# An LSTM step cut into two halves of each quarter's units

## The chip, the cores and the metric

The kernel runs on one core of a Trainium2 chip. A core has five engines that work side by side and are held together by semaphores: TensorE (matrix products; PE in the profile, with PEld for the loading of its weights), VectorE (DVE), ScalarE (ACT), GpSimd (POOL) and SyncE (SP, which here issues the DMA transfers). The metric is the device time of one execution in microseconds (us), as a median of several runs.

## The reference, cut to what matters

The model has two layers over 32 graphs of 512 nodes with 256 features: a graph attention, a Mamba-2 block, a second graph attention, and last a recurrence (an LSTM) with gated prefix and suffix sums. The change is in the recurrence. Its inputs are swapped, so that the 512 nodes are its time steps for a batch of 32:

```python
x_proj = jnp.einsum('btd,gd->btg', x, W_ih) + b_ih + b_hh
def step(carry, xp):
    h, c = carry
    gates = xp + h @ W_hh.T
    i, f, g, o = jnp.split(gates, 4, axis=-1)
    c = jax.nn.sigmoid(f) * c + jax.nn.sigmoid(i) * jnp.tanh(g)
    h = jax.nn.sigmoid(o) * jnp.tanh(c)
    return ((h, c), h)
...
logits = jnp.einsum('bth,lh->btl', lstm_out, W_lin) + b_lin
g = argmax(logits, axis=-1)[..., None]
w = g * lstm_out
inc = jnp.cumsum(w, axis=1)
prefix = inc - w
suffix = inc[:, -1:, :] - inc
return 2.0 * lstm_out + prefix * fw_att + suffix * bw_att
```

Here `x` is the layer-normalised output of the attention, and the result is added to it. Everything is in float32.

## The kernel before, in words

**The stages.** `layers_per_batch` works through the 32 graphs and takes the first 3.4 ms; a scheduler sets the order of its instructions. Beside it, `recurrence_weights` (L1030) lays the LSTM's weights out anew, with POOL and with DMAs on SP's queue, in the first 150 us, and leaves them in DRAM as `wr`. `recurrence` (L1110) then loads them as `wall` and runs the 512 steps. At the end the sums are added to the result and written out.

**The layout of a step.** The 256 units are cut into four quarters (`Q = 4`) of `J = 64`. A tile of the recurrence has 128 partitions: quarter times 32 graphs. Along a partition lie the columns of that quarter's gates: 64 each of f, i, g, o, and two more for the logits (`W = 258`). Sigmoids are made from tanh, so that one function serves all gates; the factors of one half are in the weights.

The state `hh` of a step is turned by a VectorE transpose of blocks of 32 x 32 (L1335). Of a quarter's 64 units, the first 32 end up in the first half of the turned tile's columns and the other 32 in the second: the product's contraction in two parts `k = 0, 1` (`DK = 2`) is a sum over the first and over the second halves of all quarters' units.

**The products.** TensorE's order is written out by hand (`manual_schedule`, as for VectorE and ScalarE), and it is in order. In a step it has:

- `h_part` (L1260): turned state times `whh`, added onto what is in PSUM. There are three banks, `PARTS`: f (64 columns), i with g (128), o with the logit's columns (66). For each bank: two parts `k` times four quarters. The four quarters take 32 of the array's columns each. A float32 product stands as two records in the profile, so this is 48 records.
- `x_part` of the next step (L1250): it puts the x side of the gates into the banks by a product of `xu` with an identity (`turner`): three banks times four quarters, 24 records. Bank f has one buffer, the others two: `bufs=(1, 2, 2)`.
- in four of sixteen steps, the turn of 128 rows of normalised x (`turn`, L1174).
- one of the `units` (L1236): 128 of the 1024 gate columns of x times `wih`, for eight steps at once (256 moving columns; four records). Eight of them, one in each of eight steps, make the `xu` of a later group of eight steps. ScalarE then brings it to SBUF with its bias (L1237). The last nine steps have none.

**The chain of a step.** tanh of the three banks on ScalarE (L1320); (f + 1) c and (i + 1) g on VectorE (L1322, L1323); the new cell (L1328); its tanh on ScalarE (L1330); the state (L1333); its transpose (L1335); then the products of the next step can start.

**Beside the chain on VectorE:** g_, the state where the logit says so (L1342), the running sum `pp` (L1345), and one `extra` per step: statistics or normalisation of a later chunk's x, or a part of the results of the chunk of sixteen steps before, on 512 columns. The loop's order on VectorE is: products, cell, state, turn, g_, pp, extra.

Of the kernel before, what the change touches and what calls it, by code (L numbers as in the profile page):

```python
# [9 lines left out]
F32 = mybir.dt.float32  # L10
# [3 lines left out]
AF = mybir.ActivationFunctionType  # L14
ALU = mybir.AluOpType
# [4 lines left out]
P = 128  # L20
# [3 lines left out]
DK = D // P  # L24
# [9 lines left out]
GB = 32  # L34
CH = 16
# [994 lines left out]
def recurrence_weights(nc, pool, a, wr):  # L1030
# [4 lines left out]


    Q, J = 4, 64
    W = 4 * J + 2
    nx, nh = DK * Q * 4 * J, DK * Q * W
    n0 = nx + nh  # L1040
    half = (0.5, 0.5, 0.5, 1.0)
    for_x, for_h = (0, 3, 1, 2), (1, 0, 3, 2)

    def tile_(p, n, tag):
        return pool.tile([p, n], F32, tag=tag, name=tag)

    def ordered(raw, n, order, s):
        t = tile_(P, W, "rwt")
        nc.gpsimd.memset(t[:n, 4 * J :], 0.0)
        for to, g in enumerate(order):  # L1050
            nc.gpsimd.tensor_scalar(t[:n, to * J : (to + 1) * J], raw[:n, g * J : (g + 1) * J], half[g] * s, None, ALU.mult)
        return t
# [18 lines left out]
    nc.gpsimd.tensor_tensor(b[0][:Q], b[0][:Q], b[1][:Q], ALU.add)  # L1071
    t = ordered(b[0], Q, for_x, 1.0)
    yield
    nc.sync.dma_start(out=wr[0][:, n0 + 2 * J + 8 : n0 + 2 * J + 9], in_=bl[:, 0:1])
    nc.sync.dma_start(out=wr[1].rearrange("o (q w) -> (o q) w", q=Q), in_=t[:Q, : 4 * J])
    yield
    nc.sync.dma_start(out=wr[0][:, n0 + 2 * J : n0 + 2 * J + 8], in_=wr[1].rearrange("o (u p) -> p (o u)", p=P))
    yield
# [9 lines left out]
    for n, (src, s) in enumerate(((a.wih, 1.0), (a.whh, 0.5))):  # L1088
        for k in range(DK):
            for q in range(Q):  # L1090
                raw = tile_(P, 4 * J, f"rwraw{q % 2}")
                cols = slice(q * 4 * J, (q + 1) * 4 * J)
                if n == 0:
                    nc.sync.dma_start(out=raw, in_=src[k * P : (k + 1) * P, cols])
                else:
                    for r in range(Q):
                        r0 = r * J + k * 32
                        nc.sync.dma_start(out=raw[r * 32 : (r + 1) * 32], in_=src[r0 : r0 + 32, cols])
                yield
                t = ordered(raw, P, (for_x, for_h)[n], s)  # L1100
                if n == 1:
                    nc.gpsimd.tensor_scalar(t[:, 4 * J : 4 * J + 1], wl[:, k : k + 1], 0.5, None, ALU.mult)
                yield
                w = (4 * J, W)[n]
                o0 = n * nx + (k * Q + q) * w
                nc.sync.dma_start(out=wr[0][:, o0 : o0 + w], in_=t[:, :w])
                yield


def recurrence(ctx, tc, c, a, X3, wr, out):  # L1110
# [3 lines left out]
    nc = tc.nc  # L1114
    T = X3.shape[0]
    Q, J = 4, 64
    W = 4 * J + 2
    G = CH // 2
    wp = ctx.enter_context(tc.tile_pool(name="rw", bufs=1))
    xp_ = ctx.enter_context(tc.tile_pool(name="rx", bufs=2))  # L1120
    st = ctx.enter_context(tc.tile_pool(name="rs", bufs=3))
    ch = ctx.enter_context(tc.tile_pool(name="rc", bufs=2))
# [6 lines left out]
    n0 = nx + nh  # L1129
    wall = wp.tile([P, n0 + 2 * J + 9], F32, name="wall")  # L1130
    wih = wall[:, :nx].rearrange("p (k u c) -> p k u c", k=DK, c=P)
    whh = wall[:, nx:n0].rearrange("p (k q w) -> p k q w", k=DK, q=Q)
    fw, bw = (wall[:, n0 + n * J : n0 + (n + 1) * J] for n in range(2))
    bcol = wall[:, n0 + 2 * J : n0 + 2 * J + 8]
    level = wall[:, n0 + 2 * J + 8 :]

    turner = wp.tile([P, P + 2], F32, name="turner")
    nc.vector.memset(turner[:, P:], 0.0)
    nc.vector.tensor_copy(turner[:, :P], c.ident)

# [42 lines left out]
    def results(t0, hh, pp):  # L1183
# [42 lines left out]
        return todo + [gathered]  # L1226

    def units(t0, xT, out_, u):


        if not u:
            out_[t0] = xp_.tile([P, 2 * Q, G * GB], F32, tag="xu", name=f"xu{t0}")
        xu = out_[t0]
        pu = psx.tile([P, G * GB], F32, tag="pu", bufs=2, name=f"pu{t0}_{u}")
        for k in range(DK):
            nc.tensor.matmul(pu, wih[:, k, u, :], xT[:, k, :], start=(k == 0), stop=(k == DK - 1))  # L1236
        return lambda: nc.scalar.activation(xu[:, u, :], pu, AF.Identity, bias=bcol[:, u : u + 1])  # L1237


    PARTS = ((0, J), (J, 3 * J), (3 * J, W))  # L1240

    def x_part(t, xu):

        pg = [
            psg.tile([P, e - s], F32, tag=f"pg{n}", bufs=(1, 2, 2)[n], name=f"pg{n}_{t}") for n, (s, e) in enumerate(PARTS)
        ]
        r = (t % G) * GB
        for p, half, (s, e) in zip(pg, (1, 0, 1), ((0, J), (0, P), (J, P + 2))):
            for q in range(Q):
                nc.tensor.matmul(  # L1250
                    p[q * GB : (q + 1) * GB, :], xu[:, 2 * q + half, r : r + GB], turner[:, s:e],
                    start=True, stop=(t == 0),
                )
        return pg

    def h_part(pg, h, parts=PARTS, start=False):
        for p, (s, e) in zip(pg, parts):
            for k in range(DK):
                for q in range(Q):
                    nc.tensor.matmul(  # L1260
                        p[q * GB : (q + 1) * GB, :], h[:, k, :], whh[:, k, q, s:e],
                        start=(start and k == 0), stop=(k == DK - 1),
                    )

    with tc.manual_schedule(engines={mybir.EngineType.PE, mybir.EngineType.DVE, mybir.EngineType.Activation}):
        nxt = [None] * 2
        stats, norms, turns = normalised(0, nxt)
        for s, e in ((0, nx), (n0, n0 + 2 * J + 9), (nx, n0)):
            nc.sync.dma_start(out=wall[:, s:e], in_=wr[0][:, s:e])
# [4 lines left out]
        xu = {}  # L1274
        for u in range(2 * Q):
            units(0, nxt[0], xu, u)()
        units(G, nxt[1], xu, 0)()
        extra, turning = [], {}
        pg = x_part(0, xu[0])
        z = st.tile([P, 5 * J], F32, tag="z", name="z0")  # L1280
        nc.vector.memset(z[:, :J], 0.0)
        pp = ch.tile([P, CH + 1, J], F32, tag="pp", name="pp0")
        nc.vector.memset(pp[:, 0, :], 0.0)
        h = hh = None
        for t in range(T + 1):
# [15 lines left out]
            if last:  # L1301

                pg = [psg.tile([P, W - 3 * J], F32, tag="pg2", name="pglast")]
                h_part(pg, h, PARTS[2:], True)
            elif t:
                h_part(pg, h)
            pgs = pg
            if not last:
# [6 lines left out]
                if g < T:  # L1315
                    turned.append(units(g, (xT if g < t0 + CH else nxt)[g // G % 2], xu, u))

                for (s0, e0), p in zip(PARTS, pgs):
                    e0 = min(e0, 4 * J)
                    nc.scalar.activation(z[:, J + s0 : J + e0], p[:, : e0 - s0], AF.Tanh)  # L1320
                ab = st.tile([P, 2 * J], F32, tag="ab", name=f"ab{t}")
                nc.vector.scalar_tensor_tensor(ab[:, :J], z[:, J : 2 * J], 1.0, z[:, :J], ALU.add, ALU.mult)  # L1322
                nc.vector.scalar_tensor_tensor(  # L1323
                    ab[:, J:], z[:, 2 * J : 3 * J], 1.0, z[:, 3 * J : 4 * J], ALU.add, ALU.mult
                )
                z2 = st.tile([P, 5 * J], F32, tag="z", name=f"z{t + 1}")
                cell = z2[:, :J]
                nc.vector.scalar_tensor_tensor(cell, ab[:, :J], 0.5, ab[:, J:], ALU.mult, ALU.add)  # L1328
                tc_ = st.tile([P, J], F32, tag="tc", name=f"tc{t}")
                nc.scalar.activation(tc_, cell, AF.Tanh, scale=0.5)  # L1330
                for f in turned:
                    f()
                nc.vector.scalar_tensor_tensor(hh[:, s, :], z[:, 4 * J :], 1.0, tc_, ALU.add, ALU.mult)  # L1333
                h = st.tile([P, DK, GB], F32, tag="h", name=f"h{t}")
                nc.vector.transpose(h.rearrange("p k b -> p (k b)"), hh[:, s, :])  # L1335
                z = z2
            if t:

                i = (t - 1) % CH
                p_, h_ = (pp_was, hh_was) if s == 0 and not last else (pp, hh)  # L1340
                g_ = st.tile([P, J], F32, tag="g", name=f"g{t}")
                nc.vector.scalar_tensor_tensor(  # L1342
                    g_, pgs[-1][:, J : J + 1].to_broadcast([P, J]), level, h_[:, i, :], ALU.is_gt, ALU.mult,
                )
                nc.vector.tensor_tensor(p_[:, i + 1, :], p_[:, i, :], g_, ALU.add)  # L1345
                if s == 0 and not last:
                    nc.vector.tensor_copy(pp[:, 0, :], p_[:, CH, :])
            if extra:
                extra.pop(0)()
        assert not extra and not turning  # L1350
# [27 lines left out]
def kernel(ctx: ExitStack, tc: tile.TileContext, a, out):  # L1378
# [5 lines left out]
    X3 = dram.tile([N, nb, D], F32, name="X3")  # L1384
    wr = dram.tile([P, DK * 4 * (256 + 258) + 2 * 64 + 9], F32, name="wr"), dram.tile([1, 4 * 256], F32, name="wrb")
    odd = const.tile([1, 1], I32, name="odd")
# [78 lines left out]
```

## Time and profile before

| | us |
|---|---|
| median of 3 runs (4828.24 to 4832.57) | 4829.85 |
| the profiled execution's own time | 4838.21 |
| its span, first to last instruction | 4836.4 |
| first to last transpose of the state (512 of them) | 3398.20 to 4770.22 |
| TensorE busy in the stretch 4100 to 4300 | 196.0 of 200 |
| VectorE busy there | 152.4 |
| ScalarE busy there | 109.5 |

A line of the profile names the source line, the engine, the operation, and the tiles as out<-in with the shape, partitions x elements. In a timeline the first column is the start and the second the duration, in us; equal instructions that follow each other are one row (x48), and its duration runs to the end of the last of them. In a list of waits the numbers are: us in total, times, longest. Records of products overlap: their ends hold the way through the array, and the next product may start well before. So a busy TensorE is not one at its limit, and the starts tell more than the durations.

### The profile page before, as it was taken

How to read it: one execution, taken by the hardware profiler on the slowest of the kernel's cores; microseconds unless marked ns; L12 is line 12 of the kernel's file. 1: busy time of each engine (PE TensorE's matmuls, PEld its weight loads, DVE VectorE, ACT ScalarE, POOL GpSimd, SP SyncE). 2: the span in 40 equal slices, each digit the busy share in tenths (PEclk: the TensorE clock that was granted, in tenths of full speed). 3: DMA queues.
4: the chain of work that ended last, by engine and by line, in shares of the span. 5: the costliest groups of instructions: out<-in, count | busy, mean ns of one | idle time of the engine just before them, and what ended most of it. 6: DMA issues, size and time to landing. Idle time of an engine off the chain costs nothing. (4 is left out here: it accounts for less than half of the span.)

```text
span 4836.4 us, 126769 instructions
## 1 busy us (share of the span) xinstructions
PE 4191.4 (87%) x52926; PEld 2651.5 (55%) x52926; DVE 3279.3 (68%) x8670; ACT 3068.7 (63%) x6724; POOL 1308.8 (27%) x1012
## 2 busy tenths in 40 slices
PE   4888888888888888888888888886999999999993
PEld 2444444444554444544445444544777777777772
DVE  3567666676666666666666666664677777777776
ACT  2677667776677767677677776764555555555552
POOL 4333343333433334333343333431000000000000
PEclk7899999999999999999999999998999999999997
DMA  3221122211222112221112211111111111111115
GB/s 109 64 67 61 55 70 66 65 62 55 67 65 69 57 60 62 71 69 57 60 59 73 69 57 60 53 44 60 37 39 42 38 43 41 41 40 39 42 39 159
DMA packets 273746, 288.34 MB, mean 60 GB/s; under 512 B 152844, under 2 KB 224488, under 8 KB 270984
## 3 DMA queue, kind: packets, MB, share of 16 engines
q1 hardware_dynamic: 269784, 270.26, 19.0%
q10 hardware_dynamic: 3216, 9.81, 0.7%
q8 instruction: 418, 6.85, 0.6%
q14 instruction: 168, 1.38, 0.1%
q0 software_dynamic: 160, 0.04, 0.0%
HBM read 226.04 MB, written 37.11 MB: 54 GB/s over the span
## 5 line engine op out<-in xcount | busy, mean ns | idle before, releaser
L1260 PEld LDWEIGHTS pg<-wall,h 128*32 128x32 f32 x24528 | 476.7, 109 | 228.5 <-DVE h L1335 226.8
L1260 PE MATMUL pg<-wall,h 128*32 128x64 f32 x24528 | 561.2, 239 | 34.6 <-DVE h L1335 10.6
L1236 PE MATMUL pu<-xTr,wall 128*128 128x256 f32 x2048 | 565.5, 399 | 0.0
L467 DVE SCALAR_TENSOR_TENSOR w<-w,adjT 128x1024 f32<-128x1024 f32 x256 | 348.2, 1381 | 247.4 <-ACT w L461 247.4
L1320 ACT ACTIVATE z<-pg 128x64 f32<-128x64 f32 (+1 forms) x1536 | 345.8, 241 | 129.9 <-PE pg L1260 90.2
L1237 ACT ACTIVATE xu<-pu,wall 128x256 f32<-128x256 f32 x512 | 243.2, 475 | 278.6 <-PE pu L1236 278.6
L743 ACT ACTIVATE g<-bc,cs 128x128 f32<-128x128 f32 x1024 | 322.0, 391 | 139.7 <-PE py L811 139.7
L693 DVE SCALAR_TENSOR_TENSOR acc<-px,convw,acc 128x511 f32<-128x511 f32 (+2 forms) x480 | 347.3, 746 | 76.6 <-ACT acc L688 68.7
L461 ACT ACTIVATE w<-rb,neg,colsa 128x512 f32<-128x512 f32 x512 | 387.5, 806 | 10.2 <-DMA rb<-linea 5.8
L1236 PEld LDWEIGHTS pu<-xTr,wall 128*128 128x128 f32 x2048 | 348.8, 190 | 63.7
L533 PE MATMUL pav<-w,hb 128*64 128x512 f32 x1024 | 352.6, 615 | 21.9 <-DVE w L467 21.9
L830 PE MATMUL po<-wc,xh 128*128 128x256 f32 x1024 | 282.8, 422 | 96.8 <-POOL xh L800 96.8
L729 POOL TENSOR_TENSOR ce<-ce,cT 128x384 f32<-128x384 f32 x128 | 185.1, 1475 | 667.2 <-ACT cT L701 650.3
L54 POOL TENSOR_SCALAR ve<-mv 128x4 f32<-128x4 f32 x32 | 6.2, 193 | 1317.5 <-DVE mv L1161 1317.5
L1250 PE MATMUL pg<-turner,xu 128*32 128x64 f32 (+2 forms) x12288 | 324.3, 238 | 0.4 <-issue 0.3
L945 PE MATMUL pov<-wb,wv 128*128 128x257 f32 x1024 | 246.2, 393 | 90.4 <-DVE wv L467 90.4
L672 PE MATMUL px<-mT,win 128*128 128x512 f32 x640 | 306.9, 610 | 0.0
L830 PEld LDWEIGHTS po<-wc,xh 128*128 128x128 f32 x1024 | 203.1, 212 | 141.4 <-POOL xh L800 111.1
L1330 ACT ACTIVATE tc<-z 128x64 f32<-128x64 f32 x512 | 131.6, 257 | 224.1 <-DVE z L1328 224.1
L945 PEld LDWEIGHTS pov<-wb,wv 128*128 128x128 f32 x1024 | 193.6, 194 | 135.3 <-DVE wv L467 105.6
L1250 PEld LDWEIGHTS pg<-turner,xu 128*32 128x32 f32 x12288 | 265.6, 110 | 3.0 <-issue 1.8
L56 POOL TENSOR_TENSOR rs<-ve,mhalf 128x4 f32<-128x4 f32 (+1 forms) x192 | 256.0, 1334 | 15.9
(245 smaller groups left out, 8615.4 us busy)
## 6 DMA issues: line engine op xcount, KB each, us to landing
bc<-line SPq DMA_DIRECT2D x128, 512.0 KB
adj<-in_adj_dram SPq DMA_DIRECT2D x32, 1024.0 KB
rb<-linea SPq DMA_DIRECT2D x64, 512.0 KB
ce<-line SPq DMA_DIRECT2D x64, 384.0 KB
x<-in_x_dram SPq DMA_DIRECT2D x32, 512.0 KB
X<-x SPq DMA_DIRECT2D x32, 512.0 KB
xt<-X SPq DMA_DIRECT2D x128, 128.0 KB
x<-X SPq DMA_DIRECT2D x128, 128.0 KB
```

Source lines behind the costliest of these rows:

```text
L461: nc.scalar.activation(w[:, t, k, :], rb[:, k, :], AF.Relu, bias=neg1, scale=cols[:, 2 * m + t, h + k : h + k + 1],)
L467: nc.vector.scalar_tensor_tensor(w[:, :, k, :], w[:, :, k, :], 1.0, edges, ALU.add, ALU.mult)
L533: nc.tensor.matmul(pa[k * HO : (k + 1) * HO, :], hb[:, j, 2 * q + k, :], w[:, t, k, :], start=(j == 0), stop=(j == NT - 1),)
L672: nc.tensor.matmul(pz, win[:, k, col : col + P], mT[:, k, :], start=(k == 0), stop=(k == DK - 1))
L693: nc.vector.scalar_tensor_tensor(acc[:, s:], pz[:, : N - s], convw[:, cc, k : k + 1], acc[:, s:], ALU.mult, ALU.add)
L743: nc.scalar.activation(g[:, i, k, :], bc[:, k, i * P : (i + 1) * P], AF.Relu, bias=cs[:, i, 2 * cc + k : 2 * cc + k + 1], scale=-1.0,)
L830: nc.tensor.matmul(po[:, i * D : (i + 1) * D], xh[:, cc, it * P : (it + 1) * P], wc[:, cc, :], start=(cc == 0), stop=(cc == NC - 1),)
L945: nc.tensor.matmul(po[:, : D + 1], ws[j // 2][:, j % 2, 0, it * P : (it + 1) * P], wb[:, j, :], start=(j == 0), stop=(j == NT - 1),)
L1236: nc.tensor.matmul(pu, wih[:, k, u, :], xT[:, k, :], start=(k == 0), stop=(k == DK - 1))
L1250: nc.tensor.matmul(p[q * GB : (q + 1) * GB, :], xu[:, 2 * q + half, r : r + GB], turner[:, s:e], start=True, stop=(t == 0),)
L1260: nc.tensor.matmul(p[q * GB : (q + 1) * GB, :], h[:, k, :], whh[:, k, q, s:e], start=(start and k == 0), stop=(k == DK - 1),)
L1320: nc.scalar.activation(z[:, J + s0 : J + e0], p[:, : e0 - s0], AF.Tanh)
```

## The change

The gates of a quarter are laid out in halves: for each half of its units, g, f and i (3 x 32 columns), and then o of all 64. The banks are now: half 0 (96 columns), half 1 (96), o with the logit's columns (66). With cell, g, f, i next to each other in a tile `z[n]` of a half, (f + 1) c and (i + 1) g are one instruction. Tanh, products, cell, cell's tanh, state and turn are made by halves; `h` is now two tiles, one for each part `k`. `h_part` runs first over part 0 in the banks of both halves, then over part 1, and over bank o last. An x block of a half has 96 rows, so `xu` is now ten blocks: eight of 96 rows and two of 128 for o; blocks 8 and 9 are made beside blocks 1 and 2, so that two of eight steps have two units. The buffers of the banks are still `(1, 2, 2)`. The small tiles have two buffers instead of three, and the extra comes between g_ and pp.

```diff
-    for_x, for_h = (0, 3, 1, 2), (1, 0, 3, 2)
+    order = (3, 1, 0, 2)
...
+        halves = t[:n, : 3 * J].rearrange("p (e g j) -> p e g j", e=2, g=3)
         for to, g in enumerate(order):
-            nc.gpsimd.tensor_scalar(t[:n, to * J : (to + 1) * J], raw[:n, g * J : (g + 1) * J], half[g] * s, None, ALU.mult)
+            dst, src = t[:n, 3 * J : 4 * J], raw[:n, g * J : (g + 1) * J]
+            if to < 3:
+                dst, src = halves[:, :, to, :], src.rearrange("p (e j) -> p e j", e=2)
+            nc.gpsimd.tensor_scalar(dst, src, half[g] * s, None, ALU.mult)
...
-    nc.sync.dma_start(out=wr[0][:, n0 + 2 * J : n0 + 2 * J + 8], in_=wr[1].rearrange("o (u p) -> p (o u)", p=P))
+    c0 = n0 + 2 * J
+    nc.sync.dma_start(out=wr[0][:, c0 : c0 + 8], in_=wr[1][:, : 8 * P].rearrange("o (u p) -> p (o u)", p=P))
+    nc.sync.dma_start(out=wr[0][:96, c0 : c0 + 8], in_=wr[1][:, :no].rearrange("o (u p) -> p (o u)", p=96))
+    nc.sync.dma_start(out=wr[0][:, c0 + 8 : c0 + 10], in_=wr[1][:, no:].rearrange("o (u p) -> p (o u)", p=P))
...
+                if n == 0:
+                    o0 = k * Q * 4 * J + q * 3 * J
+                    nc.sync.dma_start(out=wr[0][:, o0 : o0 + 3 * J], in_=t[:, : 3 * J])
+                    o0 = k * Q * 4 * J + no + q * J
+                    nc.sync.dma_start(out=wr[0][:, o0 : o0 + J], in_=t[:, 3 * J : 4 * J])
...
-    st = ctx.enter_context(tc.tile_pool(name="rs", bufs=3))
+    st = ctx.enter_context(tc.tile_pool(name="rs", bufs=2))
...
+    BLOCKS = [(96 * n, 96) for n in range(2 * Q)] + [(96 * 2 * Q + P * n, P) for n in range(Q // 2)]
...
+        c0, m = BLOCKS[u]
         for k in range(DK):
-            nc.tensor.matmul(pu, wih[:, k, u, :], xT[:, k, :], start=(k == 0), stop=(k == DK - 1))
-        return lambda: nc.scalar.activation(xu[:, u, :], pu, AF.Identity, bias=bcol[:, u : u + 1])
+            nc.tensor.matmul(pu[:m], wih[:, k, c0 : c0 + m], xT[:, k, :], start=(k == 0), stop=(k == DK - 1))
+        return lambda: nc.scalar.activation(xu[:m, u, :], pu[:m], AF.Identity, bias=bcol[:m, u : u + 1])
...
-    PARTS = ((0, J), (J, 3 * J), (3 * J, W))
+    PARTS = ((0, 3 * H), (3 * H, 6 * H), (6 * H, W))
...
             psg.tile([P, e - s], F32, tag=f"pg{n}", bufs=(1, 2, 2)[n], name=f"pg{n}_{t}") for n, (s, e) in enumerate(PARTS)
         ]
         r = (t % G) * GB
-        for p, half, (s, e) in zip(pg, (1, 0, 1), ((0, J), (0, P), (J, P + 2))):
+        for n, p in enumerate(pg):
+            for q in range(Q):
+                if n < 2:
+                    lhs, rhs = xu[:96, 2 * q + n, r : r + GB], c.ident[:96, :96]
+                else:
+                    lhs, rhs = xu[:, 2 * Q + q // 2, r : r + GB], turner[:, q % 2, :]
+                nc.tensor.matmul(p[q * GB : (q + 1) * GB, :], lhs, rhs, start=True, stop=(t == 0))
+        return pg
+
+    def h_part(pg, h, order, start=False):
+
+        for k, n in order:
+            p, (s, e) = pg[n], PARTS[n]
             for q in range(Q):
...
-                h_part(pg, h)
+                h_part(pg, h, ((0, 0), (0, 1), (1, 0), (1, 1), (0, 2), (1, 2)))
...
-                    turned.append(units(g, (xT if g < t0 + CH else nxt)[g // G % 2], xu, u))
...
+                    for v in (u,) + {1: (8,), 2: (9,)}.get(u, ()):
+                        turned.append(units(g, (xT if g < t0 + CH else nxt)[g // G % 2], xu, v))
+
+                for n in range(2):
+                    nc.scalar.activation(z[n][:, H:], pgs[n][:, : 3 * H], AF.Tanh)
+                zo = st.tile([P, J], F32, tag="zo", name=f"zo{t}")
+                nc.scalar.activation(zo, pgs[2][:, :J], AF.Tanh)
+                z2 = [st.tile([P, 4 * H], F32, tag=f"z{n}", name=f"z{n}_{t + 1}") for n in range(2)]
+                for n in range(2):
+                    ab = st.tile([P, 2 * H], F32, tag=f"ab{n}", name=f"ab{n}_{t}")
+                    nc.vector.scalar_tensor_tensor(ab, z[n][:, 2 * H : 4 * H], 1.0, z[n][:, : 2 * H], ALU.add, ALU.mult)
+                    nc.vector.scalar_tensor_tensor(z2[n][:, :H], ab[:, :H], 0.5, ab[:, H:], ALU.mult, ALU.add)
+                tcs = []
+                for n in range(2):
+                    tcs.append(st.tile([P, H], F32, tag=f"tc{n}", name=f"tc{n}_{t}"))
+                    nc.scalar.activation(tcs[n], z2[n][:, :H], AF.Tanh, scale=0.5)
                 for f in turned:
                     f()
...
+                for n in range(2):
+                    part = hh[:, s, n * H : (n + 1) * H]
+                    nc.vector.scalar_tensor_tensor(part, zo[:, n * H : (n + 1) * H], 1.0, tcs[n], ALU.add, ALU.mult)
+                    h.append(st.tile([P, GB], F32, tag=f"h{n}", name=f"h{n}_{t}"))
+                    nc.vector.transpose(h[n], part)
...
+            if extra and not last:
+                extra.pop(0)()
+            if t:
                 nc.vector.tensor_tensor(p_[:, i + 1, :], p_[:, i, :], g_, ALU.add)
                 if s == 0 and not last:
                     nc.vector.tensor_copy(pp[:, 0, :], p_[:, CH, :])
-            if extra:
-                extra.pop(0)()
```

## The prediction

> **What bounds the kernel now.** First the page's totals and its clock row, then the windows view (the granted clock is 1.00 in each stretch from 3500 to 4700 us, so a TensorE time read there needs no correction), then the waits of 3500 to 4800 us, then the timeline of single steps. The change touches the recurrence alone, which runs from the first to the last turn of the state:
>
> ```profile
> span 4836.4 us, 126769 instructions
> PE 4191.4 (87%) x52926; PEld 2651.5 (55%) x52926; DVE 3279.3 (68%) x8670; ACT 3068.7 (63%) x6724; POOL 1308.8 (27%) x1012
> ...
> 3398.20 0.24 DVE L1335 STREAM_TRANSPOSE h<-hh 128x64 f32<-128x64 f32 x1
> ...
> 4770.22 0.24 DVE L1335 STREAM_TRANSPOSE h<-hh 128x64 f32<-128x64 f32 x1
> ```
>
> That is 1372.0 us for 511 steps, 2.685 us each, 28% of the span. The waits name the chain's links:
>
> ```profile
> PEld pg L1260 <- DVE h L1335: 210.5, 468, 1.3
> ACT tc L1330 <- DVE z L1328: 207.3, 473, 0.7
> DVE hh L1333 <- ACT tc L1330: 182.0, 473, 0.7
> ACT z L1320 <- PE pg L1260: 84.3, 486, 1.1
> ```
>
> So TensorE waits for the turned state 0.45 us a step. That looks like room. One plain step, in order of time (columns: start, duration, engine), says how much is real:
>
> ```profile
> 4035.12 1.10 PE L1260 MATMUL pg<-wall,h 128*32 128x64 f32 x48
> 4035.68 0.22 ACT L1320 ACTIVATE z<-pg 128x64 f32<-128x64 f32 x1
> 4036.04 0.63 PE L1250 MATMUL pg<-turner,xu 128*32 128x64 f32 x24
> 4036.06 0.45 ACT L1320 ACTIVATE z<-pg 128x128 f32<-128x128 f32 x2 [0.15 <-PE pg L1260]
> 4036.59 1.13 PE L1236 MATMUL pu<-xTr,wall 128*128 128x256 f32 x4
> ```
>
> And a step in which a block of x is also turned:
>
> ```profile
> 4024.37 1.10 PE L1260 MATMUL pg<-wall,h 128*32 128x64 f32 x48
> 4025.28 0.63 PE L1250 MATMUL pg<-turner,xu 128*32 128x64 f32 x24
> 4025.84 0.44 PE L1174 MATMUL pxt<-ident,xt 128*128 128x128 f32 x2
> 4026.12 1.03 PE L1236 MATMUL pu<-xTr,wall 128*128 128x256 f32 x4
> 4027.07 1.10 PE L1260 MATMUL pg<-wall,h 128*32 128x64 f32 x48
> ```
>
> By starts, this turn step is 0.91 + 0.56 + 0.28 + 0.95 = 2.70 us of TensorE back to back, and lasts 2.70. The state's products follow 0.08 before the recorded end of the unit (4026.12 + 1.03). Put the same 0.08 on the plain step: 0.92 (state) + 0.55 (x) + 1.05 (unit) = 2.52 us of its 2.67. Chain and TensorE are nearly equal bounds: a plain step has 0.15 us of TensorE to spare, not 0.45, and a turn step has none.
>
> **The change, part by part.** Built, the changed program keeps every step's 24 state and 12 x products, with the same column totals (96 + 96 + 66 instead of 64 + 128 + 66), four quarters side by side.
>
> *The chain gets shorter.* 0 is the start of the second half's products, when the first half's are done. Records go four at a time, 0.056 us apart for 64 columns and 0.109 for 128, so about 0.083 for 96. Before, the tanh came 0.37 after the start of the bank's last group (the fourth, 0.19; tanh at 35.68 - 35.12 = 0.56); with 96 columns 0.39. So tanh 0 starts at 0.08 + 0.39 = 0.47. It takes 0.25 (223 ns for 64, 278 for 128 columns). Then VectorE: a 64-wide product 0.225; cells, states and turns of 32 columns by the slope from 225 ns (64) to 685 (512), 1.03 ns a column: 0.19, 0.19, 0.21; tanh of a half cell 0.23. Gaps as before: ACT to DVE 0.03, within DVE 0.035, DVE to ACT 0.094, DVE to PE 0.06. First half turned: 0.75 + 0.225 + 0.035 + 0.19 + 0.094 + 0.23 + 0.03 + 0.19 + 0.035 + 0.21 = 2.0; second half, a product and a cell behind: 2.37, so TensorE could go on at 2.43, against 2.67. That 0.24 is the gain on offer.
>
> *TensorE cannot take it.* First, bank 0 still has one buffer (`bufs=(1, 2, 2)`). The next step's x products start with that bank, so they wait for tanh 0. Before, it had read bank f by 0.78 after the state's start, and x came at 0.92 unhindered. Now bank 0 is complete with the sixth of its groups: tanh 0 at 5 x 0.083 + 0.39 + 0.02 (the first group's slower start) = 0.83 after the state's first product, read by 1.08, x at 1.13: a new stall of 0.21 us in every step. The release from ACT to PE is not in the trace; its nearest rows are ACT to DVE 0.03, DVE to PE 0.06, PE to ACT 0.13; I take 0.05, ends 0.03 and 0.13. Queued behind the waiting x products, in order: the transposes, the units and the next state products. Plain step: 2.52 + 0.21 = 2.73. Turn step: 2.70 + 0.21 = 2.91.
>
> *Ten units for eight.* 96 rows of a unit cost the same 256 moving columns as 128. In two of eight steps a second unit goes on TensorE: four records, 0.216 apart (their starts in the run of units before the loop), 0.86 us; such a step takes 3.59. Nothing covers it, since TensorE already sets the plain step. The unit's own ACT instruction (475 ns) lies beside that.
>
> The Trainium skill, page "TensorE: Matmul & The Clock Gate", section "LDWEIGHTS (loading the stationary operand)", puts a weight load at columns / 1.2 ns, so 96 columns load 27 ns sooner than 128, an estimate from the page; no row has 96. If one load per plain unit were exposed, the total would be some 13 us lower by it.
>
> *VectorE: three more instructions.* In the plain step's timeline:
>
> ```profile
> 4035.27 0.23 DVE L1345 TENSOR_TENSOR pp<-pp,g 128x64 f32<-128x64 f32 x1
> 4035.41 0.68 DVE L1207 TENSOR_TENSOR x<-x,m 128x512 f32<-128x512 f32 x1
> ...
> 4037.24 0.23 DVE L1333 SCALAR_TENSOR_TENSOR hh<-z,tc 128x64 f32<-128x64 f32 x1 [0.38 <-ACT tc L1330]
> 4037.49 0.24 DVE L1335 STREAM_TRANSPOSE h<-hh 128x64 f32<-128x64 f32 x1
> ```
>
> Independent neighbours start 0.14 us apart, though the first lasts 0.23; dependent ones 0.26. The step's sequence by starts: four dependent pairs 0.26 + 0.26 + 0.23 + 0.23, six independent starts of 0.10 to 0.16 (0.77), one 512-wide extra 0.60: about 2.35, under 2.73. So they cost nothing while TensorE sets the step; without that cover, still nothing until 2.43. If halves cost as much as wholes, add 0.2: still covered.
>
> Against this speaks the Trainium skill, page "VectorE: DVE Perf Modes", section "The DRAIN you can't avoid": the next instruction does not start until the pipe is empty. The rows disagree (0.14 against 0.23). By that rule durations would add up to about 2.9 a step, VectorE would bind and the total would be near 5030.
>
> *The rest, at nothing:* the third tanh of ACT and the second cell tanh (0.2 us of an engine busy 55%); the extra moved ahead of pp (VectorE alone; with it the four result stores go to SP's queue 0.3 us sooner); pools of two instead of three (the built waits are on work of two steps before); memset. Eleven more DMA issues at 0.35 to 0.66 us sit on SP's queue in the first 150 us, one behind the landing of another; loads of the first batches stand behind them: 0 to 12 (11 issues and the 4.8 us of the one landing waited for there before), taken 1, since these loads are made two batches ahead. The built order of the layers differs only in the first batches, where transposes come sooner among the mask products; the longest wait of products there was 4.3 us: -4 to 4, taken 0.
>
> **Sum.** Sixteen steps have 8 plain, 4 turn and 4 double ones: 8 x 2.73 + 4 x 2.91 + 4 x 3.59 = 47.8 us, against 16 x 2.685 = 43.0: +4.88. 503 steps carry units: 503 / 16 x 4.88 = +153. The last 9, without units, gain 0.24 each: -2. Two more units before the loop: +2. Start: +1. Total +154 on the profiled execution's 4838.2 us: 4992. That run stands 8.4 above the median of 4829.85, so the forecast is **4984 us**.
>
> **Rivals.** *No stall* (the release is hidden, or bank 0 is read sooner): plain 2.52, turn 2.70, double 3.38; 503 x 0.21 = 106 less, 4878. For it: x waited for nothing before. Against: the wait is in the built program, 0.21 past the point where TensorE runs dry. *The other side, faster:* TensorE idles 0.09 us where 128-column weights follow 32-column ones and 0.09 where it changes back. If both gaps and the stall close up, a plain step needs 2.34 and the chain's 2.43 sets it: 8 x 2.43 + 4 x 2.52 + 4 x 3.20 = 42.3, 0.64 less in sixteen, 20 us faster, 4810. It decides when the plain step is under 2.42: 16 x 2.42 + 4 x 0.18 + 4 x 0.86 is today's 43.0. Against: the gaps stand in the steps shown, and turn steps pay them. *Longer release:* at 0.13, tanh at the 128-column time, x 0.32 late: +55, 5040. *Four-wide x products lost* (their weights now have 96 of 128 rows, no row shows that): eight products of 96 columns one after the other, 4 x 0.083 become 16 x 0.083, +1.0 a step, about 5480. The built program gives them the same 128 x 32 places in the array as before, so 3 in 100.
>
> **How the numbers follow.** TensorE with the stall 0.72, forecast 4984; no or half a stall 0.10; longer release or a slower VectorE 0.10; four-wide lost 0.03; faster 0.04; nothing 0.01. The known bounds give 4984 - 25 (release 0.03, tanh at 223 ns) and + 55; the range takes in half of the no-stall case: 4905 to 5045. A difference under 0.2% (10 us) is about what a measurement of this kernel can't tell from none: faster 0.04, same 0.01, slower 0.95.
>
> **What would show it.** Right: waits of PE on the tanh of bank 0 (some 100 us in total), waits for the turned state near zero, steps of 2.73, 2.91 and 3.59 in a 2:1:1 mix, x products starting 1.13 after the state's. Wrong: state waits remain, x follows at 0.92, double steps under 3.4, or VectorE's idle before the product near zero.

## The result

| | before | after |
|---|---|---|
| median of 4 runs, us | 4829.05 (4824.08 to 4832.57) | 4996.73 (4991.89 to 5003.92) |
| the profile's span, us | 4836.4 | 4992.3 |
| first to last turn of the state | 3398.20 to 4770.22: 1372.0 | 3386.95 to 4925.95: 1539.0 |

The changed kernel takes 1.0349 times as long, with an interval of 1.0336 to 1.0362. The recurrence grew by 167 us; the layers ahead of it ended 11 us sooner, and the span is 155.9 longer.

### The profile page after: what moved, and what is told of

Same layout as the page of the kernel before. It is cut to its first block, busy times and chain, and to the rows that moved or that the text cites. A ratio compares the mean times of both kernels' runs of the same rounds, so it can differ in the third digit from the quotient of the medians.

```text
span 4992.3 us, 131522 instructions
## 1 busy us (share of the span) xinstructions
PE 4368.4 (88%) x53438; PEld 2722.9 (55%) x53438; DVE 3444.2 (69%) x10207; ACT 3211.3 (64%) x7364; POOL 1306.6 (26%) x1012
## 5 line engine op out<-in xcount | busy, mean ns | idle before, releaser
L1256 PE MATMUL pu<-xTr,wall 128*96 128x256 f32 (+1 forms) x2560 | 666.7, 392 | 0.0
L1282 PE MATMUL pg<-wall,h 128*32 128x96 f32 x24528 | 564.3, 239 | 5.0 <-DVE h L1362 5.0
L1257 ACT ACTIVATE xu<-pu,wall 96x256 f32<-96x256 f32 (+1 forms) x640 | 302.0, 472 | 347.0 <-PE pu L1256 345.6
L467 DVE SCALAR_TENSOR_TENSOR w<-w,adjT 128x1024 f32<-128x1024 f32 x256 | 347.9, 1379 | 251.5 <-ACT w L461 251.5
L1256 PEld LDWEIGHTS pu<-xTr,wall 128*96 128x96 f32 (+1 forms) x2560 | 394.8, 168 | 108.6
L1349 DVE SCALAR_TENSOR_TENSOR ab<-z 128x64 f32<-128x64 f32 x1024 | 226.6, 221 | 278.9 <-ACT z L1343 278.6
L1354 ACT ACTIVATE tc<-z 128x32 f32<-128x32 f32 x1024 | 234.6, 229 | 174.9 <-DVE z L1350 105.0
L1343 ACT ACTIVATE z<-pg 128x96 f32<-128x96 f32 x1024 | 213.4, 251 | 136.4 <-PE pg L1282 136.2
L1274 PE MATMUL pg<-ident,xu 96*32 96x96 f32 x8192 | 275.3, 252 | 17.1 <-ACT z L1343 2.4
```

Of the source, the lines that this page charges most:

```text
L467: nc.vector.scalar_tensor_tensor(w[:, :, k, :], w[:, :, k, :], 1.0, edges, ALU.add, ALU.mult)
L1256: nc.tensor.matmul(pu[:m], wih[:, k, c0 : c0 + m], xT[:, k, :], start=(k == 0), stop=(k == DK - 1))
L1257: return lambda: nc.scalar.activation(xu[:m, u, :], pu[:m], AF.Identity, bias=bcol[:m, u : u + 1])
L1274: nc.tensor.matmul(p[q * GB : (q + 1) * GB, :], lhs, rhs, start=True, stop=(t == 0))
L1282: nc.tensor.matmul(p[q * GB : (q + 1) * GB, :], h[k], whh[:, k, q, s:e], start=(start and k == 0), stop=(k == DK - 1))
```

## The profile after

The page's totals and the shares of the chain that ended last, by engine:

```profile
span 4992.3 us, 131522 instructions
PE 4368.4 (88%) x53438; PEld 2722.9 (55%) x53438; DVE 3444.2 (69%) x10207; ACT 3211.3 (64%) x7364; POOL 1306.6 (26%) x1012
...
PE 30%; DVE 1%; issue 0%; ACT 0%; DMA 0%; DVEq 0%; POOL 0%; SPq 0%; ACTq 0%
```

This last line read PE 14%, DVE 9%, ACT 4% before. Where the chain used to go round through TensorE, ScalarE and VectorE in each step, it now goes almost through TensorE alone. Next, the waits of 3500 to 4900 us (us in total, times, longest):

```profile
PEld pg L1274 <- ACT z L1343: 92.0, 464, 0.5
PEld pg L1282 <- DVE h L1362: 81.1, 226, 0.4
PEld pg L1282 <- DVE g L1370: 40.9, 114, 0.4
PEld pg L1282 <- DVE pp L1376: 35.5, 107, 0.3
```

The first line is new: in every step the x products (L1274) wait for a tanh (L1343). Before, no such wait was among the long ones. The other three lines together are 0.35 us a step (157.5 in 447 waits), and must be read with care. They seem to say that TensorE's weight loads still wait for the state. But the releaser is only the last event before the load, and two of the three, g and pp, are nothing that these products read. The timeline shows the truth. Three steps in it (start, duration, engine): one with two units (eight records of L1256), one with a turn of x (L1190), and, after the line of dots, a plain one with the start of the next. Only the rows that matter are shown; the x products of bank o, a row of their own between L1274 and what follows, are among those left out:

```profile
4089.03 1.11 PE L1282 MATMUL pg<-wall,h 128*32 128x96 f32 x48
4090.16 0.54 PE L1274 MATMUL pg<-ident,xu 96*32 96x96 f32 x16
4090.75 1.97 PE L1256 MATMUL pu<-xTr,wall 128*96 128x256 f32 x8
4092.64 1.10 PE L1282 MATMUL pg<-wall,h 128*32 128x96 f32 x48
4093.78 0.54 PE L1274 MATMUL pg<-ident,xu 96*32 96x96 f32 x16
4094.36 0.44 PE L1190 MATMUL pxt<-ident,xt 128*128 128x128 f32 x2
4094.64 1.03 PE L1256 MATMUL pu<-xTr,wall 128*96 128x256 f32 x4
4095.59 1.10 PE L1282 MATMUL pg<-wall,h 128*32 128x96 f32 x48
...
4101.29 1.10 PE L1282 MATMUL pg<-wall,h 128*32 128x96 f32 x48
4102.12 0.42 ACT L1343 ACTIVATE z<-pg 128x96 f32<-128x96 f32 x2 [0.25 <-PE pg L1282]
4102.43 0.54 PE L1274 MATMUL pg<-ident,xu 96*32 96x96 f32 x16
4103.01 1.10 PE L1256 MATMUL pu<-xTr,wall 128*96 128x256 f32 x4
4103.44 0.21 DVE L1362 STREAM_TRANSPOSE h<-hh 128x32 f32<-128x32 f32 x1
4103.58 0.19 DVE L1360 SCALAR_TENSOR_TENSOR hh<-zo,tc 128x32 f32<-128x32 f32 x1
4103.80 0.21 DVE L1362 STREAM_TRANSPOSE h<-hh 128x32 f32<-128x32 f32 x1
4104.04 0.94 PEld L1282 LDWEIGHTS pg<-wall,h 128*32 128x32 f32 x48 [0.36 <-DVE h L1362]
4104.05 1.10 PE L1282 MATMUL pg<-wall,h 128*32 128x96 f32 x48
```

In the plain step, the first half of the state is turned by 4103.65, and the products take it at 4104.05. The second half is turned by 4104.01; its products come four groups of 0.083 later, at about 4104.38. With 0.06 for the way from VectorE, each half lies ready for about 0.3 us. So it is TensorE's own queue, the unit (L1256), that is late. The state waits for TensorE and no longer TensorE for the state.

The second thing to see is the stretch from 4102.12 to 4102.43. The tanh of half 0 starts 0.83 after the state's first product and takes 0.25 (251 ns in the page's groups), and x follows at 1.14. Before, x came at 0.92.

The third is the price of the second unit: the eight records of 4090.75 hold TensorE until 4092.64, 1.89 us, where the four of the plain step hold it for 1.04. The two steps shown ahead of the plain one last 3.61 and 2.95. The medians over the recurrence, step by step of sixteen:

| step | before | after |
|---|---|---|
| plain | 2.67 | 2.75 |
| with a turn | 2.71 | 2.95 |
| with two units | (none) | 3.62 |
| the last nine, without units | 2.67 | 2.44 |

## The experiments

The theory on trial: two things make the kernel slower, the wait of the x products for bank 0's tanh and the two extra units, both on TensorE; the shorter chain is real but covered. The rival: the chain itself (the turned state, VectorE's longer list) sets the step, and the wait at bank 0 is only where idle time happens to lie. Four kernels (bank 0 last, eight units, the longer chain, and both edits) were run beside each other (the kernel before: 4827.02), the other three on another occasion (4827.36).

### The x products of bank 0 put last

```diff
-        for n, p in enumerate(pg):
+        for n in (1, 2, 0):
+            p = pg[n]
             for q in range(Q):
```

> The changed kernel with the x products in the order half 1, o, half 0, so that the bank with one buffer comes last. Theory (TensorE sets every step, and waits 0.21 us a step for the tanh of bank 0): half 0's x products come 1.2 us after the state's, later than the 1.14 at which the bank is read, so the wait goes; steps of 2.54 (plain), 2.74 (turn) and 3.40 (double); 503 x 0.21 = 106 us less, about 4891 us. Rival (the state's chain or VectorE stands right behind the wait): the wait moves to the turned state, 4960 us or more.

Measured: 4875.61 (4873.16 to 4880.81), 1.0103 of before (1.0086 to 1.012). The steps are 2.52 plain, 2.72 with a turn and 3.38 with two units. The recurrence is 1423.1, 115.9 less than in the changed kernel. The list of waits has next to nothing of the x products waiting for a tanh:

```profile
PEld pg L1275 <- ACT z L1344: 1.3, 7, 0.2
```

The timeline of a plain step:

```profile
4103.24 1.10 PE L1283 MATMUL pg<-wall,h 128*32 128x96 f32 x48
4104.15 0.36 PE L1275 MATMUL pg<-ident,xu 96*32 96x96 f32 x8
4104.32 0.31 PE L1275 MATMUL pg<-turner,xu 128*32 128x66 f32 x8
4104.44 0.35 PE L1275 MATMUL pg<-ident,xu 96*32 96x96 f32 x8
4104.73 1.10 PE L1256 MATMUL pu<-xTr,wall 128*96 128x256 f32 x4
4105.76 0.46 PE L1283 MATMUL pg<-wall,h 128*32 128x96 f32 x12
```

The x products start 0.91 after the state's, and by the time bank 0's turn comes, its tanh has read it. The wait thus costs 0.23 us in every step, 503 x 0.23 = 116 us. The time is 15 below the expected 4891: 10 of it because the wait was 0.23 and not 0.21, and 5 because the first turn of the state came sooner (3382.2 against 3386.95). The order of the banks alone takes the wait away, so it does not belong to the halves as such. That a second buffer for bank 0 would do the same is not shown: no run gave it one.

### Eight units instead of ten

The gate columns of x are cut into eight blocks of 128: g, f, i of a half, and 32 columns of o. The o bank is then filled by two products for each quarter, of 66 columns (the first half's o and zeros elsewhere) and of 32 (the second half's).

```diff
-    BLOCKS = [(96 * n, 96) for n in range(2 * Q)] + [(96 * 2 * Q + P * n, P) for n in range(Q // 2)]
+    BLOCKS = [(P * n, P) for n in range(2 * Q)]
...
-                    lhs, rhs = xu[:, 2 * Q + q // 2, r : r + GB], turner[:, q % 2, :]
...
+                    nc.tensor.matmul(pg[2][rows, :], xu[:, 2 * q, r : r + GB], turner, start=True, stop=False)
+            if n == 2:
+                for q in range(Q):
+                    nc.tensor.matmul(
+                        pg[2][q * GB : (q + 1) * GB, H:J], xu[:, 2 * q + 1, r : r + GB], c.ident[:, 3 * H :],
+                        start=False, stop=(t == 0),
+                    )
...
-                    for v in (u,) + {1: (8,), 2: (9,)}.get(u, ()):
+                    for v in (u,):
```

> The changed kernel with eight units of 128 rows: a half's block of x holds its 96 columns of g, f, i and its 32 of o, and the o bank gets them by two products (66 and 32 columns). Theory (TensorE sets every step): the double steps go, -0.86 us in four of sixteen; the o bank's extra x products cost 0.06 in every step; plain 2.81, turn 3.01; 12 x 2.81 + 4 x 3.01 = 45.8 against 48.3 in sixteen steps, about 79 us less, 4918 us. Rival (second units lie beside waits): 4990 us or more.

Measured: 4921.49 (4920.23 to 4930.19), 1.0194 of before (1.0177 to 1.0211). The long steps are gone; plain steps are 2.84, turn steps 3.01. The recurrence takes 1468.6, 70 less than in the changed kernel. The wait at bank 0 is still there:

```profile
PEld pg L1267 <- ACT z L1346: 81.1, 416, 0.5
```

The plain step was 0.03 dearer than expected. Its timeline says why:

```profile
4076.20 0.54 PE L1267 MATMUL pg<-ident,xu 128*32 128x96 f32 x16
4076.56 0.30 PE L1271 MATMUL pg<-turner,xu 128*32 128x66 f32 x8
4076.67 0.24 PE L1274 MATMUL pg<-ident,xu 128*32 128x32 f32 x8
4076.85 1.13 PE L1251 MATMUL pu<-xTr,wall 128*128 128x256 f32 x4
4077.91 1.10 PE L1285 MATMUL pg<-wall,h 128*32 128x96 f32 x48
```

The x products take 0.65 by starts instead of 0.58, and the unit of 128 columns 1.06 instead of 1.04. So the extra units cost 125.75 steps x 0.87 = 109 us, and this way of avoiding them costs some 39 of it back.

### A longer chain

One more dependent VectorE instruction of 32 columns between half 0's state and its turn. VectorE works in order, so half 1 comes later too.

```diff
+                        tmp = st.tile([P, H], F32, tag="tmp", name=f"tmp{t}")
+                        nc.vector.scalar_tensor_tensor(tmp, zo[:, :H], 1.0, tcs[0], ALU.add, ALU.mult)
+                        nc.vector.tensor_scalar(part, tmp, 1.0, None, ALU.mult)
```

> The changed kernel with one more dependent VectorE instruction of 32 columns (a product with 1.0) between the first half's state and its turn: the chain of both halves gets 0.23 us longer. Theory (the chain is off the path, both halves' states come 0.33 us before TensorE takes them): 4997 us, within 5, but for the last nine steps (+2). Rival (the chain sets part of the time): up to 503 x 0.23 = 116 us more, 5113 us.

Measured: 4996.41 (4989.06 to 5000.89), 1.0346 of before (1.0327 to 1.0366). The steps are 2.75, 2.95 and 3.61, as they were. Only the last nine, which have no units, grew: from 2.44 to 2.63. So the instruction does lengthen the chain, by 0.19, and in the 503 other steps nobody waits for it. The rival falls. With it falls the plain reading of the list of waits, in which 0.35 us a step stands against the state.

### Three more instructions in the chain

The same place, with three dependent instructions.

> The changed kernel with three more dependent 32-column VectorE instructions instead of one between half 0's state and its turn, 0.69 us on the chain. Theory (TensorE's order of work with the stall sets the step, the turned halves lie about 0.33 us ready before TensorE takes them): the first 0.33 are free, the rest is paid in plain steps, less in turn steps (0.2 longer), nothing in double ones: plain 2.75 + 0.36 = 3.11, turn 2.95 + 0.16 = 3.11, double 3.62; 503/16 x (8 x 0.36 + 4 x 0.16) = 110, and the last nine 0.65 each, 6: 5113. Rival (the chain had no such slack and one more instruction merely hid elsewhere): the whole 0.69 in 16 steps of 16, 350 us, 5347; rival (the chain never matters): 4997.

Measured: 5095.72 (5092.75 to 5098.18), 1.0557 of before (1.0541 to 1.0573). Plain and turn steps are both 3.06, steps with two units 3.62 as before, and the last nine 3.06. Three instructions lengthen the chain by 0.62 (3.06 - 2.44), not 0.69; 0.31 of that is free in a plain step. That is the room seen in the timeline, and the list of waits now has the wait that it lacked, of the products themselves and not of their weight loads:

```profile
PEld pg L1282 <- DVE h L1371: 170.9, 281, 0.9
...
PE pg L1282 <- DVE h L1371: 46.2, 187, 0.5
```

### Both: eight units, and bank 0 last

> The changed kernel with both edits: bank of half 0 last in the x products, and eight units. Theory (both are work of TensorE and add up): plain 2.59, turn 2.79; 12 x 2.59 + 4 x 2.79 = 42.2 in sixteen steps against 48.3 of the changed kernel and 43.0 before: about 4807 us, faster than before by some 0.5%. Rival (the gains overlap, or the chain at 2.44 plus a wait now shows): 4870 us or more. The layers' part, which ended 11 us sooner in the changed kernel, has the old order of weight transfers here: if that order made the 11 us, the first turn of the state comes at about 3398 us again and the total is 4818.

Measured: 4809.64 (4808.77 to 4811.96), **0.9964 of before (0.995 to 0.9978)**. Steps are 2.60 plain and 2.78 with a turn, the recurrence 1356.8. The halves of the step are thus worth something once both prices are gone: the recurrence is 15 us shorter than before. (The profiled executions are 26.2 apart, 4810.2 against 4836.4; the other 11 lie ahead of the first turn.) The two edits add up to within 4 us: 115.9 and 70 taken off one by one would have left 1353. The expectation also named a test of the layers: if the order of the transfers had made the 11 us, the first turn would come at about 3398 again with the transfers of before. It came at 3387.5.

### Both, and no column of o written twice

```diff
-                    nc.tensor.matmul(pg[2][rows, :], xu[:, 2 * q, r : r + GB], turner, start=True, stop=False)
+                    nc.tensor.matmul(pg[2][rows, :H], xu[:, 2 * q, r : r + GB], turner[:, :H], start=True, stop=False)
...
-                        pg[2][q * GB : (q + 1) * GB, H:J], xu[:, 2 * q + 1, r : r + GB], c.ident[:, 3 * H :],
+                        pg[2][q * GB : (q + 1) * GB, H:], xu[:, 2 * q + 1, r : r + GB], turner[:, : H + 2],
```

> The kernel of both edits (bank 0 last, eight units), with the o bank's two x products of 66 and 32 columns made 32 and 34 columns, so that no column is written twice. Theory (TensorE's own work sets each step of that kernel): in its plain step the two groups of 66 columns take 0.11 us by their starts (4101.07 to 4101.18), those of 32 take 0.06 (4101.18 to 4101.24); so 0.05 less a step, plain 2.55 instead of 2.60, turn 2.73 instead of 2.78, 503 x 0.05 = 25 us: 4785 against 4810. Rival (a load of eight new weights, not the columns, paces these short products, or the chain is already the bound): 4810, steps of 2.60 as they were.

Measured: 4791.15 (4783.18 to 4795.3), **0.9928 of before (0.9914 to 0.9941)**, the fastest of all. Steps are 2.55 and 2.73. The plain step's timeline:

```profile
4099.76 1.10 PE L1285 MATMUL pg<-wall,h 128*32 128x96 f32 x48
4100.68 0.35 PE L1267 MATMUL pg<-ident,xu 128*32 128x96 f32 x8
4100.84 0.25 PE L1271 MATMUL pg<-turner,xu 128*32 128x32 f32 x8
4100.90 0.25 PE L1274 MATMUL pg<-turner,xu 128*32 128x34 f32 x8
4100.97 0.35 PE L1267 MATMUL pg<-ident,xu 128*32 128x96 f32 x8
4101.25 1.13 PE L1251 MATMUL pu<-xTr,wall 128*128 128x256 f32 x4
4102.31 1.10 PE L1285 MATMUL pg<-wall,h 128*32 128x96 f32 x48
```

The 0.05 us that the columns promised came out of the median step in full. The recurrence is 1334.1 against 1356.8, 22.7 less, of the 25 that 503 x 0.05 would make. TensorE's own work sets this kernel's plain step as well.

### Both, with the longer chain

> The kernel of both edits with the one dependent VectorE instruction of 0.23 us between half 0's state and its turn. Theory (with the stall and the double steps gone, the chain stands right behind TensorE: in a plain step half 0's turn ends at 4102.34 and half 1's at 4102.70, and TensorE takes them at 4102.59 and about 4102.92, so 0.19 and 0.16 are spare after 0.06 for the way): 0.07 late in plain steps, nothing in turn steps; plain 2.67 instead of 2.60, turn 2.78; 12 of 16 steps, 503 x 0.75 x 0.07 = 26 us, the last nine 0.19 each: 4838. Rival (the chain has as much room as in the changed kernel, where 0.23 cost nothing): 4812. Rival (the chain is already the bound): 0.23 in each step, 4925.

Measured: 4828.87 (4825.52 to 4840.32), 1.0006 of before (0.9996 to 1.0015). Plain steps are 2.63 and turn steps 2.78; the last nine are 2.63 too, so here the chain is the bound of the plain step. In the timeline the state's products follow the first half's turn by 0.05:

```profile
4065.08 0.21 DVE L1370 STREAM_TRANSPOSE h<-hh 128x32 f32<-128x32 f32 x1
4065.34 1.10 PE L1285 MATMUL pg<-wall,h 128*32 128x96 f32 x48
4065.39 0.21 DVE L1370 STREAM_TRANSPOSE h<-hh 128x32 f32<-128x32 f32 x1
```

The expected 2.67 was too much because the instruction adds 0.19 and not 0.23. The room in the kernel of both edits is 2.60 - 2.44 = 0.16, as was read from the timeline.

## Why the prediction was right

The time, its sign and its mechanism came as forecast: 4984 against 4996.73. The terms of the sum, and what the runs make of each:

| | forecast | measured | by |
|---|---|---|---|
| steps with neither price (2.52 plain, 2.72 with a turn), against 2.685 | -60 | -58 | bank 0 last |
| the stall at bank 0 | +106 | +116 | bank 0 last |
| the second unit in 4 of 16 steps | +108 | +109 | step medians |
| the last nine steps | -2 | -2 | step medians |
| rest of the recurrence | 0 | +2 | what is left |
| all ahead of the first turn of the state | +3 | -11 | first turn of the state |
| sum | +155 | +156 | |

The measured rows make up 167 for the recurrence, where 151 was forecast, and -11 ahead of it. (The forecast's first row is 503 / 16 x (12 x 2.52 + 4 x 2.70 - 16 x 2.685); the measured one has 2.72; the forecast's own sum, from rounded steps, was +154.) The profiled execution took 4994.07 against 4992 forecast. The 12.7 between the medians' forecast and the median are nearly all in how the profiled executions stand to their medians: 8.4 above before, 2.7 below after.

**What bounds the kernel.** "A plain step has 0.15 us of TensorE to spare, not 0.45": confirmed. TensorE's plain step was put at 2.52 from two timelines of the kernel before, and is 2.52 once the wait is gone. Its parts were off and cancelled: x takes 0.58 by starts instead of 0.55, the unit 1.03 instead of 1.05.

**The chain.** The sum gave 2.43; the last nine steps, where nothing else is in the way, take 2.44. The tanh of 96 columns was put at 0.25 and takes 0.251, its start at 0.83 and it is 0.83. That each half would be turned with room to spare was shown by adding to the chain: 0.19 more cost nothing, 0.62 more cost 0.31.

**The stall.** 0.21 was forecast and 0.23 measured: the release from ScalarE to TensorE takes 0.06 rather than 0.05 (tanh read by 4102.37, x at 4102.43), and the state's products are done at 0.91 rather than 0.92. This is the rival "no stall" refuted in the trace, and then made true by the order of the banks: 4878 had been worked out for it, and the kernel with bank 0 last took 4875.61.

**Ten units for eight.** The step with two was put at 3.59 and is 3.62, the second unit 0.87 instead of 0.86; the other 0.02 is the stall.

**VectorE.** Its three more instructions cost nothing, as forecast. The forecast set against that a rule from the Trainium skill's page "VectorE: DVE Perf Modes", section "The DRAIN you can't avoid", and estimated about 2.9 us of VectorE in a step by it. It read only half of that section, which goes on: "A next op that is not held starts earlier". The rows agree with this half: the transpose of 4103.44 lasts 0.21, and the state's second half starts at 4103.58, 0.14 later. The fastest kernel above, which keeps all of VectorE's instructions, runs plain steps of 2.55. On ScalarE the forecast counted one instruction too many: three tanhs of banks stand in each step of both kernels, and only the second cell's tanh is new. Neither changed the sum.

**The weight loads.** The page "TensorE: Matmul & The Clock Gate", section "LDWEIGHTS (loading the stationary operand)", has 96 columns load 27 ns sooner than 128; the forecast set 13 us apart for it and took none. The groups of the changed kernel's matrix loads, 3500 to 4700 us, now show both widths (the number behind x is the count, then us in total and mean ns):

```profile
L1256 PEld LDWEIGHTS pu<-xTr,wall 128*96 128x96 f32 x1588 | 229.2, 162 | 70.0
L1256 PEld LDWEIGHTS pu<-xTr,wall 128*128 128x128 f32 x400 | 76.0, 190 | 13.0
```

The difference, 162 against 190 ns, is 28 and agrees with the page. The durations do not: the page's formula, columns / 1.2 ns, would make them 80 and 107. In plain steps the unit is 0.02 to 0.03 shorter by starts with 96 columns (1.03 and 1.04 against 1.06), which is what one exposed load per plain step would make; which load it is, no run shows. In turn steps it is not seen: 0.95 in the changed kernel, 0.95 in the kernel before.

**The other rivals.** "The other side, faster" needed the idle 0.09 us at a change between 32-column and 128-column weights to close up. It did not: the unit of a turn step still takes 0.95, and four records of 0.216 are 0.86. "Longer release" fell with the release of 0.06, and "four-wide x products lost" with x products of 96 rows that take 0.17 for two groups of four records.

**Signs that were named.** Steps of 2.73, 2.91 and 3.59 came as 2.75, 2.95 and 3.62; x at 1.13 came at 1.14; waits for the tanh of "some 100 us" came as 92.0. "Waits for the turned state near zero" failed as a sign: the list shows 81.1 against h. It was the sign that was wrong, not the step: that entry stands before the weight loads whatever the chain does, as the longer chain showed.

**The mis-sized terms.** The layers were put at -4 to 4, plus 0 to 12 for the transfers and 2 for the units before the loop; the first turn came 11 us sooner. That is 14 from the value taken and outside the bounds. The recurrence missed by 16 the other way, 10 of them the stall of 0.23 for 0.21. That the sum came out within 2 us is luck in this one place: two misses of 14 and 16 cancelled.

**What stays open.** Whether the order of the weights' transfers brought those 11 us. The third graph's mask products (L467) start at 226.3 in the changed kernel and at 224.5 to 227.1 in the three others with its transfers. They start at 236.6 before, and at 230.3 to 235.4 in the four with as few transfers as before. So the transfers, by their order or their number, seem to do something early, some 3 to 12 us. But the first turn of the state comes at 3382.2 to 3390.3 in the first group and at 3381.0 to 3398.2 in the second. One profile each can't tell an effect of 10 us at the end of the layers from their own wander.

## What to carry to other kernels

Cutting a chain in two pays only if the engine that the chain hands over to has the idle time; add up that engine's work by the starts of its records, step kind by step kind, before counting on a wait that the profile lists. When a buffer's reader moves later in the step, look at the writer that comes next and at the number of buffers: here one line that puts that bank last gave back 116 us. A block cut to 96 rows for the sake of a layout costs as much as one of 128 when the time goes by moving columns, so keep the number of blocks and pay elsewhere: with both mended the halves beat the kernel before by 0.4%, and by 0.7% with no column of o written twice.

## What the runs showed of the hardware

- Products with the four quarters side by side go by their columns down to 32: two groups take 0.17 us for 96 columns, 0.11 for 66, 0.06 for 32 or 34 (by starts). Weights of 96 rows instead of 128 make no difference: 0.17 for two groups in both (4104.15 to 4104.32 with bank 0 last; 4100.90 to 4101.07 in the kernel of both edits, whose timeline is not shown).
- A dependent VectorE instruction of 32 columns takes about 0.22 us of a chain: its own 182 ns and 0.034 of gap. With three more in the chain, the rows of one of the last nine steps are:

```profile
5013.15 0.18 DVE L1365 TENSOR_SCALAR tm<-tmp 128x32 f32<-128x32 f32 x1
5013.36 0.18 DVE L1365 TENSOR_SCALAR tm<-tm 128x32 f32<-128x32 f32 x1
5013.58 0.18 DVE L1367 TENSOR_SCALAR hh<-tm 128x32 f32<-128x32 f32 x1
5013.80 0.21 DVE L1371 STREAM_TRANSPOSE h<-hh 128x32 f32<-128x32 f32 x1
```

The slope from 64 and 512 columns had said 0.19 and a gap of 0.035. The last nine steps grew by 0.03 less than the rows say (0.19 for one, 0.62 for three). Beside that stands that their state products last 1.13 in the changed kernel, where they also wait for the second half, and 1.10 with one or three more instructions.

- An idle stretch of at least 0.33 us of the weight loader before the state's products stands in every kernel of this study (0.33 to 0.36 in most steps where these products wait for nothing), with whatever ended last as its releaser: h, hh, g, pp, statistics, or "issue". Only what goes beyond it was a wait for the state here: the median is 0.47 in the kernel before, where a plain step had 0.15 of TensorE to spare, and 0.67 with three more instructions in the chain, where plain steps grew by 0.31. Where this list named tiles that the instruction doesn't read, it was no wait for data.
